# Attention scores and maxima as 128-row matmuls, the negated maximum as two of the rows

## The chip, the core and the metric

The kernel runs on one core of a Trainium2 chip as a single program. The metric is the device time of one execution in microseconds (us). Engines are named as the profile names them: PE is TensorE's matmuls and PEld its weight loads, DVE is VectorE, ACT is ScalarE, POOL is GpSimd, and SP is the engine whose queue issues nearly all DMAs.

## What is computed

A layer norm and an attention block with 16 heads of 16 dimensions over four sequences of 1024 tokens and 256 channels, then a ternary feed-forward, a memory layer that scans over the tokens, and the feed-forward again. The change touches only the softmax of the attention:

```python
qkv = (h @ w_qkv + b_qkv).reshape(B, T, 3, NUM_HEADS, HEAD_DIM)      # B 4, T 1024, 16 heads of 16
scores = jnp.einsum('bhqd,bhkd->bhqk', q, k) / np.sqrt(HEAD_DIM)
attn = jax.nn.softmax(scores, axis=-1)
out = jnp.einsum('bhqk,bhkd->bhqd', attn, v)
...
x = x + _L0_attn_a_ref(_layernorm(x, axis=-1), ...)
x = x + _L0_ffn_ref(_layernorm(x, axis=-1), L0_ffn_weight)
x = x + _L0_attn_b_ref(_layernorm(x, axis=-1), ...)
x = x + _L0_ffn_ref(_layernorm(x, axis=-1), L0_ffn_weight)
```

## The kernel before

**Numbers in two halves.** Queries and keys are kept as a rounded float32r part ("hi") and the rest ("lo"), written to DRAM (dq, dk) by `project`. A product of a query and a key is one float32r matmul with 64 rows: 16 dimensions times two parts of the query times two parts of the key. The 64 rows of one head stand in the slots by repeating the loads: `load_keys` writes each key row to two rows of a slot (`kslot`), `load_queries` does likewise for queries (`qslot`). Two heads (s = 0, 1) lie below each other in the 128 rows, and two such pairs (p = 0, 1) side by side, so that a slot holds four heads.

**Tiling.** A unit is one block of 256 queries (L34), one sequence b and two groups of four heads. A unit has two parts, one for each group; there are 32 units and 64 parts (L183 to L191). A part goes through the 1024 keys in eight steps kc of 128 keys. One such step is a call of `half` (L1219):

- `maxima` (L229) for a part that lies 12 steps ahead: two matmuls with queries as weights and 512 keys streaming, one for each half of the rows, into a tile of 1024 columns; then one VectorE reduction (L239) to the negated maximum over those keys. Eight such steps make a part's maxima.
- `scores` (L266): for the two pairs of heads, two matmuls each with 128 keys as weights and 256 queries streaming (L273), one for each half of the rows; then for each half a matmul of a matrix of ones with `mslot` (L278), which adds the negated maximum to the scores; then two exponentials on ScalarE (L281) into `pt`.
- `maxima_rows` (L241), once in eight steps: the eight negated maxima per query are split into two parts that sum to them, transposed, written to DRAM (d, four DMAs) and loaded into rows 0, 1 and 64, 65 of `mslot`, whose other rows are zero (two DMAs).

`weigh` (L285) then multiplies `pt` with the values: four float32 matmuls, each on 32 columns of the array; the machine runs a float32 matmul as two passes, so there are eight instructions. They accumulate over all steps of a unit in one PSUM bank (`av`), which VectorE copies out at the unit's end (L301), and `settle` divides by the softmax sums through DRAM.

**PSUM.** Of eight banks, four hold two maxima tiles, one `av`, and three rotate through all other work (`mps`, pool "m"): two for each step of scores before the change.

**What sets the order.** PE, DVE and ACT run in the order of the source text (`manual_schedule`, L975); SP and POOL are ordered by the framework. `part` (L1245) places the loads and calls `half` for each kc, then `beside(PACE)`, which issues pieces of the other work (projections of the next sequences, output projections, feed-forward, memory layer) up to an allowance counted in PE columns: 1200 per step, saved up to 1500, and at most 700 in one step once begun. After it come the value products: of this and earlier steps, if the other work was light (under 500 columns) or kc is odd.

```python
half(v, kc)
light = beside(PACE) < LIGHT
while late and (light or kc % 2):
    weigh_late()
late.append((v, kc))
```

**Slots and leads.** There are six key slots (three parts), four query slots and two for the maxima rows. In `part(v)`, keys are loaded at kc 1 and 5 (L1248, L1256), queries at kc 2 for part v + 3 (L1252), values at kc 2. A key slot serves both the maxima and, 12 steps later, the scores. `rest` (L1287) uses the slots as spare tiles when the attention has ended.

**The start.** `load_x`, constants, memsets of the slots that must hold zeros or ones (L1012 to L1016), then projection of the first sequence with loads in between (L1352 to L1359), then 12 steps of maxima alone.

Of the kernel before, what the change touches and what calls it, by code (L numbers as in the profile page):

```python
# [17 lines left out]
P = 128  # L18
# [3 lines left out]
SL = 32  # L22
# [15 lines left out]
def tile_hybrid(ctx: ExitStack, tc: tile.TileContext, x, ln_gamma, ln_beta, w_qkv, b_qkv, w_out, b_out,  # L38
# [22 lines left out]
    dq = [drk.tile([NG, 2, 2, HD, 2, S], F32, name=f"dq{b}") for b in range(B)]  # L61
    dk = [drk.tile([NG, 2, 2, 2, HD, S], F32, name=f"dk{b}") for b in range(B)]
# [114 lines left out]
    kslots = [slp.tile([P, 2, N5], F32R, tag=f"kslot{i}", name=f"kslot{i}") for i in range(6)]  # L177
    qslots = [slp.tile([P, 2, N5 // 2], F32R, tag=f"qslot{i}", name=f"qslot{i}") for i in range(4)]
    mslots = [slp.tile([P, N5], F32R, tag=f"mslot{i}", name=f"mslot{i}") for i in range(2)]
    ngs = [slp.tile([P, SL], F32, tag=f"ng{i}", name=f"ng{i}") for i in range(2)]  # L180
    ones = slp.tile([P, P], F32R, tag="ones", name="ones_r")
# [10 lines left out]
    W = N5 // 2  # L192
    vals, kS, qS = {}, {}, {}

    def load_keys(v, hf):

        if v >= len(parts) or (v, hf) in kS:
            return
        u, e = parts[v]
        k, b, gs = units[u]  # L200
        kt = kS[v, hf] = kslots[(2 * v + hf) % len(kslots)]
        src = dk[b][gs[e]].rearrange("p s h d n -> (s h d) p n")[:, :, hf * N5 : (hf + 1) * N5]
        to = kt.bitcast(F32).rearrange("(x r) p n -> x r p n", r=2)
        for r in range(2):
            nc.sync.dma_start(to[:, r], src)

    def load_queries(v):
# [7 lines left out]
        for s in range(2):  # L215
            src = dq[b][gs[e], :, s, :, :, t0 : t0 + W].rearrange("p d r n -> (d r) p n")
            for h in range(2):
                o = HR * s + SL * h
                nc.sync.dma_start(q.bitcast(F32)[o : o + SL], src)
# [9 lines left out]
    def maxima(v, n):  # L229

        hf, p, j = n // 4, n // 2 % 2, n % 2
        kt = kS[v, hf]
        if v not in nms:
            nms[v] = ngp.tile([P, 2, 2, 2, 2], F32, tag="nm", name=f"nm_{v}")
        ps = pools["x"].tile([P, 2, N5], F32, tag="x", name=f"mx_{v}_{n}")
        for s in range(2):
            r = slice(HR * s, HR * (s + 1))
            T.matmul(ps[:, s, :], lhsT=qS[v][r, p, j * P : (j + 1) * P], rhs=kt[r, p, :], start=True, stop=True)  # L238
        V.tensor_reduce(nms[v][:, hf, :, p, j], ps, AX.X, ALU.max, negate=True)  # L239

    def maxima_rows(v):  # L241
# [3 lines left out]
            out=nx, in0=nms[v][:, 0].rearrange("p s i j -> p (s i j)"),  # L245
# [728 lines left out]
    with ExitStack() as by_hand:  # L974
        by_hand.enter_context(tc.manual_schedule(engines=OWN))  # L975
        share(m=8)
        with ExitStack() as s1_:
# [35 lines left out]
            for t in mslots:  # L1013
                G.memset(t.bitcast(F32), 0.0)
# [426 lines left out]
```

## Time and profile before

| | us |
|---|---|
| median of 3 runs | 1516.4 (1515.99 to 1517.36) |
| the profiled execution | 1527.27 |
| its span, first to last instruction | 1525.5 |
| mean granted TensorE clock | 0.917 |

| stage of the profiled execution | us |
|---|---|
| before the first maxima | 0 to 52 |
| first score product to last | 72 to 1400 |
| the rest (end of the memory layer, outputs) | 1400 to 1525 |

A row of the page's costliest groups holds the line, the engine and operation, the tile written and those read, the shapes (`64*128` is rows times columns of the array in use), the count, the busy time of the group in us (overlaps counted once), the mean duration of one in ns, and the idle time of the engine just ahead of them with what ended it. A row of the timeline holds the start in us, the length of a run of equal instructions from first start to last end, engine, line, tiles, shape and count. Ends of matmuls are modelled, so that starts are what the intervals are read from. The granted clock (PEclk) is 1.00 or 0.50 at any moment.

The DMA engines moved 165.94 MB in 128657 packets and were busy 34.1% for the SP queue:

```profile
## 3 DMA queue, kind: packets, MB, share of 16 engines
q1 hardware_dynamic: 128252, 163.39, 34.1%
```

### The profile page before, as it was taken

The numbers are of one execution on the slowest core, as the hardware profiler recorded it, in microseconds if no ns is written. First come the engines' busy times: TensorE is split into PE (matmuls) and PEld (weight loads), VectorE is DVE, ScalarE is ACT, GpSimd is POOL, SyncE is SP. The second block draws the span as 40 slices with busy tenths as digits, with TensorE's granted clock in tenths as the row PEclk, the third lists the DMA queues.
The fourth block names the chain that finished last, engine by engine and source line by source line (L and its number), as shares of the span: only waits on it lengthen the run. The fifth ranks groups of instructions, "written<-read, shape, count | busy, mean of one in ns | idle before, by whom it ended". The sixth has DMA issues, their size and how long they took to land.

```text
span 1525.5 us, 27625 instructions
## 1 busy us (share of the span) xinstructions
PE 1333.4 (87%) x10496; PEld 790.4 (52%) x10496; DVE 1045.1 (69%) x1768; ACT 786.3 (52%) x1477; POOL 235.2 (15%) x434
## 2 busy tenths in 40 slices
PE   6469999999997897999988898999998888998786
PEld 3235455554554554655544554655545545654564
DVE  5656667587787657668778658678868568573564
ACT  2134536466666454566666454466654554565333
POOL 4331102000001103110002103110002113010233
PEclk9679999999999897999999898999998999999778
DMA  6536544544434222233443222334442222231001
GB/s 200 181 111 198 154 158 129 178 156 147 143 119 129 77 67 73 77 115 126 136 149 101 66 64 88 100 103 135 152 136 64 94 70 76 93 102 43 1 9 33
DMA packets 128657, 165.94 MB, mean 109 GB/s; under 512 B 33868, under 2 KB 76172, under 8 KB 128524
## 3 DMA queue, kind: packets, MB, share of 16 engines
q1 hardware_dynamic: 128252, 163.39, 34.1%
q8 instruction: 83, 1.36, 0.4%
q10 hardware_dynamic: 272, 0.79, 0.1%
q14 instruction: 50, 0.41, 0.1%
HBM read 123.24 MB, written 38.76 MB: 106 GB/s over the span
## 4 chain that ended last, share of the span: by engine, by line
PE 56%; DVE 22%; ACT 8%; DMA 6%; SPq 3%; issue 3%; POOL 2%; DVEq 0%; ACTq 0%; POOLq 0%
PE av L294 12%; PE mx L238 9%; DVE nm L239 8%; PE sc L273 6%; PE sc L278 6%; ACT pt L281 3%; PE cps L1139 2%; PE opf L874 2%; PE pf L390 2%; PE po L390 2%; DMA d<-nt 2%; PE gps L818 1%; PE vps L1162 1%; DMA dk<-lo 1%; PE qqps L540 1%
## 5 line engine op out<-in xcount | busy, mean ns | idle before, releaser
L281 ACT ACTIVATE pt<-sc 128x512 f32<-128x512 f32 x1024 | 555.7, 594 | 501.5 <-PE sc L278 500.0
L239 DVE TENSOR_REDUCE nm<-mx 128x2 f32<-128x1024 f32 x512 | 617.5, 1218 | 138.5 <-PE mx L238 131.6
L294 PE MATMUL av<-pt,v 128*32 128x256 f32 x4096 | 333.9, 413 | 30.3 <-DVE a L301 30.2
L238 PE MATMUL mx<-kslot,qslot 64*128 64x512 f32 x1024 | 275.1, 520 | 26.4 <-DVE lo L1144 15.3
L273 PE MATMUL sc<-qslot,kslot 64*128 64x256 f32 x2048 | 237.1, 295 | 27.6 <-DVE kqm L634 14.8
L273 PEld LDWEIGHTS sc<-qslot,kslot 64*128 64x128 f32 x2048 | 220.7, 196 | 59.1 <-ACT pt L281 19.2
L278 PE MATMUL sc<-mslot,ones_r 64*128 64x512 f32 x1024 | 226.2, 412 | 15.5 <-DMA mslot<-d 15.3
L238 PEld LDWEIGHTS mx<-kslot,qslot 64*128 64x128 f32 x1024 | 102.8, 191 | 249.8 <-issue 129.9
L294 PEld LDWEIGHTS av<-pt,v 128*32 128x32 f32 x4096 | 91.2, 112 | 169.5 <-issue 114.0
L278 PEld LDWEIGHTS sc<-mslot,ones_r 64*128 64x128 f32 x1024 | 113.7, 196 | 18.5 <-DMA mslot<-d 9.9
L72 POOL TENSOR_TENSOR rso_hn<-rsi_hn,nhalf 128x2 f32<-128x2 f32 (+1 forms) x17 | 11.9, 699 | 332.0 <-DVE rsi_hn L71 332.0
L1139 PE MATMUL cps<-hT,wg 128*128 128x512 f32 x128 | 62.6, 629 | 0.1
L1144 DVE SCALAR_TENSOR_TENSOR lo<-cps,bqk,hi 128x512 fp32r<-128x512 f32 x32 | 23.9, 751 | 54.8 <-ACT hi L1143 44.4
L1143 ACT ACTIVATE hi<-cps,bqk 128x512 fp32r<-128x512 f32 x32 | 22.0, 688 | 51.8 <-PE cps L1139 26.1
L1139 PEld LDWEIGHTS cps<-hT,wg 128*128 128x128 f32 x128 | 23.9, 199 | 28.5 <-issue 25.7
L874 PE MATMUL opf<-ffn,ohT 128*128 128x256 f32 x128 | 33.2, 404 | 5.1 <-ACT ohT L869 5.1
L72 POOL TENSOR_TENSOR rso_hd<-rsi_hd,nhalf 128x2 f32<-128x2 f32 (+1 forms) x17 | 11.9, 700 | 158.8 <-DVE rsi_hd L71 146.7
L1180 POOL TENSOR_SCALAR X<-X,rr_a 128x256 f32<-128x256 f32 x32 | 18.6, 591 | 111.7 <-DVE h L1121 111.7
L557 DVE SCALAR_TENSOR_TENSOR vk<-rvk,cw_vk,vk 128x512 f32<-128x512 f32 x21 | 15.8, 752 | 28.5 <-ACT vk L555 28.0
L390 PE MATMUL po<-wo,aT 128*128 128x256 f32 x128 | 35.2, 419 | 0.0
L818 PE MATMUL gps<-gwT,hid 128*128 128x256 f32 x128 | 33.7, 408 | 0.5 <-ACT pt L281 0.5
L301 DVE COPY a<-av 128x512 f32<-128x512 f32 x32 | 21.8, 683 | 16.7 <-PE av L294 16.6
(358 smaller groups left out, 1583.6 us busy)
## 6 DMA issues: line engine op xcount, KB each, us to landing
kslot<-dk SPq DMA_DIRECT2D x256, 256.0 KB
v<-dv SPq DMA_DIRECT2D x32, 604.0 KB
qslot<-dq SPq DMA_DIRECT2D x256, 64.0 KB
da<-a SPq DMA_DIRECT2D x31, 256.0 KB
dv<-vtile SPq DMA_DIRECT2D x8, 604.0 KB
X<-in_L_attn_a_x_dram SPq DMA_DIRECT2D x8, 512.0 KB
dq<-hi SPq DMA_DIRECT2D x16, 256.0 KB
dq<-lo SPq DMA_DIRECT2D x16, 256.0 KB
```

The source lines that it names most:

```text
L72: G.tensor_tensor(out=r[:, :n], in0=t[:, :n], in1=nhalf[:, :n], op=ALU.pow)
L238: T.matmul(ps[:, s, :], lhsT=qS[v][r, p, j * P : (j + 1) * P], rhs=kt[r, p, :], start=True, stop=True)
L239: V.tensor_reduce(nms[v][:, hf, :, p, j], ps, AX.X, ALU.max, negate=True)
L273: T.matmul(ps[s][:, p * W : (p + 1) * W], lhsT=kt[r, p, o : o + P], rhs=qS[v][r, p, :], start=p == 0, stop=False, skip_group_check=True,)
L278: T.matmul(ps[s], lhsT=ones[r, :], rhs=mslots[v % 2][r, :], start=False, stop=True, skip_group_check=True)
L281: A.activation(pt[:, s, :], ps[s], AF.Exp, scale=1.0 / HD**0.5)
L294: T.matmul(avs[u][SL * i : SL * (i + 1), e * W : (e + 1) * W], lhsT=vt[:, kc, o : o + SL], rhs=pt[:, i % 2, i // 2 * W : (i // 2 + 1) * W] ...
L390: T.matmul(ps[:, e, :], lhsT=srcT[:, cc, e, :], rhs=w[:, cc, :], start=cc == 0, stop=cc == 1)
L818: T.matmul(ps[:, e, :], lhsT=hidT[:, cc, p.start + e, :], rhs=gwT[:, cc, :], start=cc == 0, stop=cc == 1)
L874: T.matmul(pf[:, e, :], lhsT=hT[:, cc, e, :], rhs=ffn[:, cc, :], start=cc == 0, stop=cc == 1)
L1139: T.matmul(ps, lhsT=wg[:, cc, n * P : (n + 1) * P], rhs=hT[:, cc, o], start=cc == 0, stop=cc == 1)
L1144: V.scalar_tensor_tensor(out=low, in0=ps, scalar=bqk[:, n : n + 1], in1=high.bitcast(F32), op0=ALU.add, op1=ALU.subtract,)
```

## The change

Line numbers ahead are those of the kernel before. Each head now has the array's 128 rows for itself: 64 rows of products as before, two rows (64 and 65) in which the query slot holds the two parts of the negated maximum and the key slot for scores holds ones, and 62 rows of zeros. So one matmul gives a score with its maximum taken off, and the separate product with the matrix of ones (L278) is gone. For maxima the key slot must hold zeros in rows 64 and 65, so keys are loaded twice, into `mslots` (two heads, 512 keys) for maxima and `sslots` (four heads, 256 keys) for scores, three slots of each, each load issued as two DMAs two pieces ahead of its use, inside `maxima` and `scores`. Query slots hold four heads side by side; there are three, loaded for part v + 2 at kc 0. DRAM layouts of dq and dk follow. `maxima_rows` writes its rows into the query slot with one load.

The order in a step changes: `scores` stand ahead of `maxima`; a step's scores go bank by bank, two products and an exponential each. Value products are issued at odd kc, and at kc 0 of a unit's first part, for all steps that are left. `PACE` is 600, `LIGHT` is gone. At the start nine slots are cleared and three pairs of rows set to one.

```diff
-    dq = [drk.tile([NG, 2, 2, HD, 2, S], F32, name=f"dq{b}") for b in range(B)]
-    dk = [drk.tile([NG, 2, 2, 2, HD, S], F32, name=f"dk{b}") for b in range(B)]
+    dq = [drk.tile([NG, 4, HD, 2, S], F32, name=f"dq{b}") for b in range(B)]
+    dk = [drk.tile([NG, 4, 2, HD, S], F32, name=f"dk{b}") for b in range(B)]
...
-    kslots = [slp.tile([P, 2, N5], F32R, tag=f"kslot{i}", name=f"kslot{i}") for i in range(6)]
-    qslots = [slp.tile([P, 2, N5 // 2], F32R, tag=f"qslot{i}", name=f"qslot{i}") for i in range(4)]
-    mslots = [slp.tile([P, N5], F32R, tag=f"mslot{i}", name=f"mslot{i}") for i in range(2)]
+    W = N5 // 2
+    qslots = [slp.tile([P, 4, W], F32R, tag=f"qslot{i}", name=f"qslot{i}") for i in range(3)]
+    sslots = [slp.tile([P, 4, W], F32R, tag=f"sslot{i}", name=f"sslot{i}") for i in range(3)]
+    mslots = [slp.tile([P, 2, N5], F32R, tag=f"mslot{i}", name=f"mslot{i}") for i in range(3)]
...
-    ones = slp.tile([P, P], F32R, tag="ones", name="ones_r")
...
+    def keys_into(t, of):
+
+        to = t.bitcast(F32)[:HR].rearrange("(x r) i n -> x r i n", r=2)
+        for r in range(2):
+            nc.sync.dma_start(to[:, r], of.rearrange("i h d n -> (h d) i n"))
+
+    def load_scored(x):
+
+        v, c = x // 4, x % 4
...
+        scored[x] = sslots[x % len(sslots)]
+        keys_into(scored[x], dk[b][gs[e], :, :, :, c * W : (c + 1) * W])
+
+    def load_maxed(y):
+
+        v, hf, p = y // 4, y // 2 % 2, y % 2
...
+        maxed[y] = mslots[y % len(mslots)]
+        keys_into(maxed[y], dk[b][gs[e], 2 * p : 2 * p + 2, :, :, hf * N5 : (hf + 1) * N5])
...
-        for s in range(2):
-            src = dq[b][gs[e], :, s, :, :, t0 : t0 + W].rearrange("p d r n -> (d r) p n")
-            for h in range(2):
-                o = HR * s + SL * h
-                nc.sync.dma_start(q.bitcast(F32)[o : o + SL], src)
+        src = dq[b][gs[e], :, :, :, t0 : t0 + W].rearrange("i d r n -> (d r) i n")
+        for h in range(2):
+            nc.sync.dma_start(q.bitcast(F32)[SL * h : SL * (h + 1)], src)
...
         hf, p, j = n // 4, n // 2 % 2, n % 2
-        kt = kS[v, hf]
+        if j == 0:
+            load_maxed(4 * v + n // 2 + 2)
+        kt = maxed[4 * v + n // 2]
...
         for s in range(2):
-            r = slice(HR * s, HR * (s + 1))
-            T.matmul(ps[:, s, :], lhsT=qS[v][r, p, j * P : (j + 1) * P], rhs=kt[r, p, :], start=True, stop=True)
+            T.matmul(
+                ps[:, s, :], lhsT=qS[v][:, 2 * p + s, j * P : (j + 1) * P], rhs=kt[:, s, :], start=True, stop=True
+            )
...
-        for s in range(2):
-            nc.sync.dma_start(
-                mslots[v % 2].bitcast(F32)[HR * s : HR * s + 2, :], d[:, s].rearrange("h x q -> h (x q)")
-            )
+        nc.sync.dma_start(
+            qS[v].bitcast(F32)[HR : HR + 2].rearrange("h i n -> h (i n)"), d.rearrange("h x q -> h (x q)")
+        )
...
-        kt, o = kS[v, kc // 4], kc % 4 * P
-        ps = [mps([P, N5], f"sc_{v}_{kc}_{s}") for s in range(2)]
-        rows = [slice(HR * s, HR * (s + 1)) for s in range(2)]
-        for p in range(2):
-            for s, r in enumerate(rows):
+        if kc % 2 == 0:
+            load_scored(4 * v + kc // 2 + 2)
+        kt, o = scored[4 * v + kc // 2], kc % 2 * P
+        pt = pts[v, kc] = ptp.tile([P, 2, N5], F32, tag="pt", name=f"pt_{v}_{kc}")
+        for x in range(2):
+            ps = mps([P, N5], f"sc_{v}_{kc}_{x}")
+            for y in range(2):
                 T.matmul(
-                    ps[s][:, p * W : (p + 1) * W], lhsT=kt[r, p, o : o + P], rhs=qS[v][r, p, :],
-                    start=p == 0, stop=False, skip_group_check=True,
+                    ps[:, y * W : (y + 1) * W], lhsT=kt[:, 2 * x + y, o : o + P], rhs=qS[v][:, 2 * x + y, :],
+                    start=True, stop=True,
                 )
-        for s, r in enumerate(rows):
-            T.matmul(ps[s], lhsT=ones[r, :], rhs=mslots[v % 2][r, :], start=False, stop=True, skip_group_check=True)
-        pt = pts[v, kc] = ptp.tile([P, 2, N5], F32, tag="pt", name=f"pt_{v}_{kc}")
-        for s in range(2):
-            A.activation(pt[:, s, :], ps[s], AF.Exp, scale=1.0 / HD**0.5)
+            A.activation(pt[:, x, :], ps, AF.Exp, scale=1.0 / HD**0.5)
...
-            G.memset(ones.bitcast(F32), 1.0)
-            for t in mslots:
+            for t in (*qslots, *mslots, *sslots):
                 G.memset(t.bitcast(F32), 0.0)
+            for t in sslots:
+                G.memset(t.bitcast(F32)[HR : HR + 2], 1.0)
...
-            LIGHT, PACE = 500, 1200
+            PACE = 600
...
                 pend = None
+                if v is not None:
+                    scores(v, kc)
                 if todo:
...
-                if v is not None:
-                    scores(v, kc)
...
-                    if kc == 1:
-                        load_keys(v + 2, 1)
-                    if kc == 2:
-                        if v + 3 < 2 * n0:
-                            through("before", lambda key: key <= units[(v + 3) // 2][1])
-                        load_queries(v + 3)
-                        if v % 2 == 0 and v // 2 + 1 < U:
-                            load_values(v // 2 + 1)
-                    if kc == 5:
-                        load_keys(v + 3, 0)
+                    if kc == 0:
+                        b = units[min(v // 2 + 1, U - 1)][1]
+                        if v + 2 < 2 * n0 and b:
+                            through("before", lambda key: key <= b)
+                        load_queries(v + 2)
+                    if kc == 4 and v % 2 == 0 and v // 2 + 1 < U:
+                        load_values(v // 2 + 1)
                     half(v, kc)
-                    light = beside(PACE) < LIGHT
-                    while late and (light or kc % 2):
-                        weigh_late()
+                    beside(PACE)
+                    if kc % 2 or v % 2 == 0 and kc == 0:
+                        while late:
+                            weigh_late()
                     late.append((v, kc))
...
-                for v in (2 * u, 2 * u + 1):
-                    load_queries(v)
-                    for hf in range(2):
-                        if v < 3:
-                            load_keys(v, hf)
+                if u == 0:
+                    for v in range(2):
+                        load_queries(v)
+                    for y in range(3):
+                        load_maxed(y)
+                    for x in range(3):
+                        load_scored(x)
```

## The prediction

> **What bounds the kernel now.** I read the page's head first, then its costliest groups, then one stretch of TensorE in order of time, then busy times by stretch, and last the SP queue.
>
> ```profile
> span 1525.5 us, 27625 instructions
> PE 1333.4 (87%) x10496; PEld 790.4 (52%) x10496; DVE 1045.1 (69%) x1768; ACT 786.3 (52%) x1477; POOL 235.2 (15%) x434
> ...
> L239 DVE TENSOR_REDUCE nm<-mx 128x2 f32<-128x1024 f32 x512 | 617.5, 1218 | 138.5 <-PE mx L238 131.6
> L294 PE MATMUL av<-pt,v 128*32 128x256 f32 x4096 | 333.9, 413 | 30.3 <-DVE a L301 30.2
> L238 PE MATMUL mx<-kslot,qslot 64*128 64x512 f32 x1024 | 275.1, 520 | 26.4 <-DVE lo L1144 15.3
> L273 PE MATMUL sc<-qslot,kslot 64*128 64x256 f32 x2048 | 237.1, 295 | 27.6 <-DVE kqm L634 14.8
> ...
> L278 PE MATMUL sc<-mslot,ones_r 64*128 64x512 f32 x1024 | 226.2, 412 | 15.5 <-DMA mslot<-d 15.3
> ```
>
> TensorE is busy 87% of the span and hardly waits for data: the idle times ahead of its four big groups add up to 100 us. All four belong to one step, which I call a half: 512 halves, each with one maxima pair (L238), four score products (L273), two products that add the negated maximum (L278) and eight value products (L294). One half in order of time (start, duration, line, count):
>
> ```profile
> 700.89 0.50 PE L238 MATMUL mx<-kslot,qslot 64*128 64x512 f32 x2
> 701.22 0.41 PE L273 MATMUL sc<-qslot,kslot 64*128 64x256 f32 x4
> 701.46 0.40 PE L278 MATMUL sc<-mslot,ones_r 64*128 64x512 f32 x2
> 701.79 0.64 PE L294 MATMUL av<-pt,v 128*32 128x256 f32 x8
> 702.36 0.50 PE L238 MATMUL mx<-kslot,qslot 64*128 64x512 f32 x2
> ```
>
> The starts tell what each group costs: 0.33 + 0.24 + 0.33 + 0.57 = 1.47 us. Four score products of 256 columns in 0.24 us are two pairs at 0.12 each, so the two 64-row tiles run at the same time. A 512-column pair should then take 0.22; the two that stand next to a change of tile shape (L238 behind `128*32`, L278 ahead of it) take 0.33, that is 0.11 more. Busy times of whole stretches (length; PE, PEld, DVE, ACT, POOL busy; granted clock, DMA share, GB/s):
>
> ```profile
> 736.50:748.60 12.10, 12.10 (x132) 6.66 (x131) 10.98 (x14) 8.69 (x17) 0.00 (x0) 1.00 0.59 193
> 597.00:614.00 17.00, 15.60 (x89) 10.52 (x91) 12.16 (x26) 5.98 (x12) 3.88 (x8) 0.50 0.14 43
> 100.00:1400.00 1300.00, 1190.08 (x9900) 694.67 (x9899) 925.26 (x1482) 731.04 (x1372) 163.81 (x288) 0.94 0.36 112
> ```
>
> The first is one part (8 halves) with hardly any other work beside it: PE full, VectorE at 91%, the DMA engines at 59%. I counted 22 of the 64 parts shorter than 16.2 us like it; the others carry projections and memory work, and PE is the bound there too.
>
> **The change, part by part.** *Streaming.* The 64-row pairs become single 128-row matmuls, one after another, and the L278 pair goes. Removed per half: 0.23 (L238, without the 0.11 for its change of shape) + 0.24 (L273) + 0.22 (L278) = 0.69 us. Added: four products of 256 columns and two of 512, in the same type. No 128-row matmul of this type is in the trace. From below, a pair's time for a single one: 4 x 0.12 + 2 x 0.22 = 0.90 us. From above, the float32 passes that do fill the array:
>
> ```profile
> 299.74 3.62 PE L1162 MATMUL vps<-wg,hT 128*128 128x256 f32 x16
> 114.56 9.99 PE L1139 MATMUL cps<-hT,wg 128*128 128x512 f32 x22
> ```
>
> Less the last one's own duration (0.38 and 0.59), these come every 0.216 us (256 columns) and 0.45 us (512), so a half would need 4 x 0.216 + 2 x 0.45 = 1.76 us. I take the lower one: the type sets the rate, since a float32 pass on `64*128` (L833, 256 columns) also starts every 0.215 us. 0.90 - 0.69 = 0.21 us a half, times 512: **+107 us**; bounds +84 (0.107 and 0.213 per product, half the float32 pass) and +548.
>
> The Trainium skill speaks against this part: "TensorE: Matmul & The Clock Gate", Part 3 (row/col tiling), states that a weight load overlaps a running matmul only where the row groups differ, and in a full array they never do. The two rows above disagree: twice the columns cost twice the time (0.45 against 0.216), so no constant weight load is in them. By the rule, with a load of 0.107 us (an estimate from that page's columns / 1.2 GHz), six loads in 512 halves would add 329 us more; the trace decides.
>
> *Changes of tile shape.* Scores and maxima now have the shape of most projections (`128*128`), and value products are issued for two halves together. In the two listed orders of instructions the shape changes 1141 times before and 715 times after, between the first maxima and the last value product. Entering `128*32` costs 0.11 + 0.02 (its first pass takes 0.24 instead of 0.22); leaving it 0.09 of drain + 0.11 of exposed weight load, 0.20; the other kinds about 0.20. Before: 429 x 0.13 + 712 x 0.20 = 198 us. After: 287 x 0.13 + 428 x 0.20 = 123 us. **-75 us**; bounds -55 and -89 (all 426 at 0.13, or at 0.21).
>
> *Negated maxima as rows of the query slot.* The chain nx, transpose, d (4 DMAs), one load instead of two (0.25 us less) stays. The rows are now needed by a half's first product and no more by L278, 0.57 us later, and the last reduction starts 0.45 us later since maxima stand behind scores. PE waited for these rows 16 times, 25.2 us in all. **+5 us** (16 times 0.3); bounds 0 and +40 (0.6 in every part). What waits behind it on PE is the rest of the half, and VectorE's reductions.
>
> *Keys loaded twice, in small pieces.* Issue times on SP (min/median/max in ns):
>
> ```profile
> L205 SPq DMA_DIRECT2D kslot<-dk x256: 580/610/1651, 35.3 to 1355.8; - x128
> L219 SPq DMA_DIRECT2D qslot<-dq x256: 303/427/1441, 32.1 to 1340.1; - x128
> ```
>
> Per part, 4 x 0.61 + 4 x 0.43 + 2 x 0.25 = 4.7 us go and 16 key loads, 2 query loads and 1 row load come: 18 x 0.52 + 0.25 = 9.6 us (0.52 is midway between the two medians: rows are strided as for kslot, but half as many), 5.7 to 11.2 at 0.30 and 0.61 each. In the 12.1 us part SP was issuing for 7.5 us by the trace; it will be at 12.4 (8.5 to 14.0). The bytes of keys per part go from 1 to 2 MB, +87 GB/s there: 193 to 280, so the DMA share goes from 0.59 to about 0.86. And a load is issued only 4 halves (5.9 us) ahead of its use, in a slot that the piece just finished had; before, 7 for keys. Behind a late key load wait, on SP, the d and query-row loads, and on PE everything. Elsewhere a part lasts 20 to 30 us and covers this. **+8 us** (0.36 in each of 22 parts); bounds 0 and +55 (2.5 in each).
>
> *At the start* POOL clears nine slots of 1024 columns and three pairs of rows: from the 128x512 rows (0.49 each) 8.8 + 2.9 us instead of 1.2, where it idled 9.29 us before L1097 (the first statistics). **+1 us**; bounds 0 and +3.
>
> *Cover and pace.* ACT's two exponentials and VectorE's reduction per half are unchanged: 1.08 and 1.22 us, still below 1.49. Other work beside a half is halved in pace (600 for 1200 columns) but all of it is still issued before the end: the PE columns after the last value product are the same (37402 and 37403). Spread thinner, it may spare waits for the copy L301 (30.2 us) or cause some in the projections, which now run in larger bursts. **0**; bounds -30 and +15.
>
> Sum: 107 - 75 + 5 + 8 + 1 = **+46 us** at rounded prices. The profiled execution took 1527.3 us, 1.8 around its span, so it would take 1573; it stands 10.9 above the median of the runs, 1516.4. The forecast for the median is 1516.4 + 46 = **1562 us**.
>
> **The rivals.** *A, faster: the clock.* Between 100 and 1400 us the granted clock is 0.94, so some 12% of 1300 us ran at half speed, costing up to 78 us. The stretch from 597 shows how: PE had idled, then worked 17 us at 0.50, while a full part has 1.00. Fewer shape changes, thinner other work and more streaming could keep it up. It decides from 0.98 on: at that, 0.04 x 1300 = 52 us come back, and 1562 - 52 = 1510; at 0.99, 1497. Against it: those stretches come from waits for VectorE's chain in the memory work, which stays. The same page of the skill, Part 1, states that the clock is halved after an idle window of about 3.4 us; if no stall of that kind went, nothing would come back.
>
> *B, slower by more: SP and the DMA engines become the bound of the short parts.* At the upper price +55 instead of +8: 1609. For it: 62% of SP's time and 59% of the DMA engines are used there already. Against it: 42 parts have time to spare.
>
> *C: the 128-row product of this type streams at the float32 pass's rate.* +548 in place of +107: about 2000. Against it, the pairs' 0.12.
>
> *D: shape changes cost more than priced*, at -89, and streaming the least, +84: 1516.4 - 5 + 14 = 1525.
>
> **How the numbers follow.** The forecast, 1540 to 1590: 0.48. D, 1519 to 1540: 0.12. B: 0.14. C: 0.02. A: 0.19. That leaves 0.05 within 0.2% (3 us), which is about what a measurement of this kernel can tell from no change. Faster 0.19, same 0.05, slower 0.76. The range leaves out C, the best of A and the worst of B: 1505 to 1610.
>
> **What would show it.** Right: score products of 256 columns start every 0.11 to 0.12 us, maxima every 0.22; a lone half at about 1.49 us against 1.47, and halves with projections shorter than before; SP busy nine tenths or more in short parts; waits of PE for the DMAs of the key slots, few and short. Wrong: products at 0.22 (C); weight loads standing between matmuls; a mean clock of 0.98 or more between 100 and 1400 us (A); PE waiting over 1 us for key slots in most short parts (B); or the shape change being dearer than 0.2 us.

## The result, and the profile after

The changed kernel takes 1657.2 us (median of 4 runs, 1654.4 to 1671.4) against 1516.2 for the kernel before: a ratio of 1.0947, 95% interval 1.0894 to 1.1001. The forecast was 1562 us, slower: the direction was right, but the forecast loss of 46 us is a third of the measured 141, and the time lies outside the range.

The profiled execution has a span of 1669.6 us. The head of its page and its costliest groups of PE and DVE:

```profile
span 1669.6 us, 26853 instructions
PE 1403.6 (84%) x9472; PEld 917.4 (55%) x9472; DVE 1046.0 (63%) x1768; ACT 779.0 (47%) x1477; POOL 248.6 (15%) x443
...
L254 DVE TENSOR_REDUCE nm<-mx 128x2 f32<-128x1024 f32 x512 | 617.6, 1218 | 317.4 <-PE mx L251 316.3
L289 PE MATMUL sc<-qslot,sslot 128*128 128x256 f32 x2048 | 407.8, 320 | 76.5 <-DMA sslot<-dk 49.0
L251 PE MATMUL mx<-mslot,qslot 128*128 128x512 f32 x1024 | 347.5, 423 | 68.6 <-DMA mslot<-dk 39.9
L306 PE MATMUL av<-pt,v 128*32 128x256 f32 x4096 | 296.8, 404 | 11.1 <-DVE a L313 11.1
```

The two key slots now head the waits of the groups that had hardly any. Two halves in order of time, the value products of two halves first:

```profile
808.00 1.07 PE L306 MATMUL av<-pt,v 128*32 128x256 f32 x16
809.00 0.74 PE L289 MATMUL sc<-qslot,sslot 128*128 128x256 f32 x4
809.57 0.63 PE L251 MATMUL mx<-mslot,qslot 128*128 128x512 f32 x2
810.04 0.71 PE L289 MATMUL sc<-qslot,sslot 128*128 128x256 f32 x4
810.59 0.62 PE L251 MATMUL mx<-mslot,qslot 128*128 128x512 f32 x2
```

Here nothing waits. From one group of 16 value products to the next such a pair of halves takes 3.16 us at the median (51 pairs at full clock), 1.58 a half against 1.47 before. Over 512 halves that would be some 55 us, so the matmuls alone are not the loss. The longest PE waits that name a DMA, in us, times and the longest one:

```profile
PE sc L289 <- DMA sslot<-dk: 49.0, 27, 4.0
PE mx L251 <- DMA mslot<-dk: 39.9, 43, 3.1
PE vkps L552 <- DMA hid<-dh: 35.3, 3, 11.9
```

The issues on SP, and the queue's share of the 16 DMA engines (34.1% before):

```profile
L199 SPq DMA_DIRECT2D mslot<-dk x512: 571/598/2948, 38.3 to 1512.1; - x171
L199 SPq DMA_DIRECT2D sslot<-dk x512: 571/602/1762, 42.3 to 1533.0; - x171
```

```profile
q1 hardware_dynamic: 203772, 230.54, 49.2%
```

All but 5 us of the loss lie between the first score product and the last: 71.8 to 1399.6 before, 76.9 to 1543.9 after; what follows takes 125.9 and 125.7 us. I cut this loop into its 64 parts at every 32nd score product, and the sums below, worked out from the records of single profiled executions, serve all that follows. "First" are parts 0 to 10, with the projections; "light" the other 20 that lasted under 16.2 us before; "mid" 12 up to 22 us; "heavy" 18 longer ones, and 20, 36, 52 the three in which a block of the memory layer begins. Idle is time without a matmul; "half speed" is length times (1 - granted clock), part by part. (A stall can count in both.)

| loop, us | all | first | light | mid | heavy | 20, 36, 52 | PE idle | half speed |
|---|---|---|---|---|---|---|---|---|
| before | 1328 | 258 | 285 | 231 | 487 | 68 | 127 | 89 |
| after | 1467 | 288 | 386 | 239 | 435 | 120 | 196 | 104 |
| e1, no reloads | 1289 | 246 | 326 | 222 | 418 | 78 | 81 | 31 |
| e5, before, no reloads | 1314 | 253 | 285 | 229 | 478 | 68 | 123 | 79 |
| e7, before, new pace | 1342 | 260 | 325 | 223 | 418 | 117 | 165 | 73 |
| e8, before, extra loads | 1448 | 268 | 324 | 288 | 501 | 67 | 216 | 136 |
| e17, before, allowance 600 | 1310 | 256 | 299 | 238 | 448 | 69 | 112 | 87 |
| e10, e1 with the old order | 1322 | 248 | 307 | 218 | 485 | 64 | 85 | 30 |
| e18, e1, value products spread | 1322 | 253 | 326 | 222 | 453 | 68 | 78 | 45 |

After against before: light parts +102, the three parts +52, the first 11 +30, heavy parts -53.

### The profile page after: what moved, and what is told of

Read it like the earlier page. It is cut to its first block, busy times and chain, and to the rows that moved or that the text cites. A ratio compares the mean times of both kernels' runs of the same rounds, so it can differ in the third digit from the quotient of the medians.

```text
span 1669.6 us, 26853 instructions
## 1 busy us (share of the span) xinstructions
PE 1403.6 (84%) x9472; PEld 917.4 (55%) x9472; DVE 1046.0 (63%) x1768; ACT 779.0 (47%) x1477; POOL 248.6 (15%) x443
## 4 chain that ended last, share of the span: by engine, by line
PE 54%; DMA 15%; DVE 13%; SPq 6%; ACT 5%; POOL 4%; issue 3%; DVEq 0%; ACTq 0%; POOLq 0%
PE sc L289 12%; PE mx L251 10%; PE av L306 9%; DMA mslot<-dk 6%; DVE nm L254 5%; SPq L199 4%; DMA sslot<-dk 3%; PE pf L402 2%; PE cps L1152 2%; PE vps L1175 2%; PE opf L886 2%; DMA da<-a 2%; PE gps L830 1%; PE po L402 1%; ACT pt L293 1%
## 5 line engine op out<-in xcount | busy, mean ns | idle before, releaser
L289 PE MATMUL sc<-qslot,sslot 128*128 128x256 f32 x2048 | 407.8, 320 | 76.5 <-DMA sslot<-dk 49.0
L289 PEld LDWEIGHTS sc<-qslot,sslot 128*128 128x128 f32 x2048 | 307.9, 198 | 244.3 <-issue 147.9
L251 PE MATMUL mx<-mslot,qslot 128*128 128x512 f32 x1024 | 347.5, 423 | 68.6 <-DMA mslot<-dk 39.9
L306 PE MATMUL av<-pt,v 128*32 128x256 f32 x4096 | 296.8, 404 | 11.1 <-DVE a L313 11.1
L251 PEld LDWEIGHTS mx<-mslot,qslot 128*128 128x128 f32 x1024 | 167.0, 200 | 84.9 <-issue 41.4
L72 POOL TENSOR_TENSOR rso_hn<-rsi_hn,nhalf 128x2 f32<-128x2 f32 (+1 forms) x17 | 14.6, 860 | 386.6 <-DVE rsi_hn L71 386.6
L552 PE MATMUL vkps<-hid,wvk 128*128 128x512 f32 x32 | 21.9, 823 | 35.3 <-DMA hid<-dh 35.3
L72 POOL TENSOR_TENSOR rso_hd<-rsi_hd,nhalf 128x2 f32<-128x2 f32 (+1 forms) x17 | 11.9, 702 | 223.7 <-DVE rsi_hd L71 210.7
L1175 PE MATMUL vps<-wg,hT 128*128 128x256 f32 x128 | 34.3, 423 | 8.4 <-DVE lo L1157 8.4
L402 PE MATMUL pf<-ffn,hnT 128*128 128x256 f32 x124 | 39.7, 477 | 0.5 <-ACT hnT L395 0.5
L1175 PEld LDWEIGHTS vps<-wg,hT 128*128 128x128 f32 x128 | 27.0, 214 | 16.1 <-DVE lo L1157 10.8
L402 PEld LDWEIGHTS pf<-ffn,hnT 128*128 128x128 f32 x124 | 30.1, 246 | 8.3 <-ACT pt L293 1.3
```

The costliest lines, as they stand in the source:

```text
L72: G.tensor_tensor(out=r[:, :n], in0=t[:, :n], in1=nhalf[:, :n], op=ALU.pow)
L251: T.matmul(ps[:, s, :], lhsT=qS[v][:, 2 * p + s, j * P : (j + 1) * P], rhs=kt[:, s, :], start=True, stop=True)
L289: T.matmul(ps[:, y * W : (y + 1) * W], lhsT=kt[:, 2 * x + y, o : o + P], rhs=qS[v][:, 2 * x + y, :], start=True, stop=True,)
L306: T.matmul(avs[u][SL * i : SL * (i + 1), e * W : (e + 1) * W], lhsT=vt[:, kc, o : o + SL], rhs=pt[:, i // 2, i % 2 * W : (i % 2 + 1) * W], ...
L402: T.matmul(ps[:, e, :], lhsT=srcT[:, cc, e, :], rhs=w[:, cc, :], start=cc == 0, stop=cc == 1)
L1175: T.matmul(ps[:, e, :], lhsT=hT[:, cc, o : o + P], rhs=wg[:, cc, 2 * C :], start=cc == 0, stop=cc == 1,)
```

## The experiments

Times are medians, followed by the ratio and its 95% interval. Ratios are to the kernel before in the same session, so compare ratios; 0.01 is 15 us.

**How much the key loads cost (e1, e2, e3, on the changed kernel).** e1 loads the slots for the first three pieces alone and leaves the later loads of keys out; e2 loads half of the columns with as many DMAs; e3 issues only the first of each two DMAs, and so leaves out the products with the queries' lower parts.

```diff
 # e1, for sslots; mslots likewise with y
+        if x < 3:
+            keys_into(scored[x], dk[b][gs[e], :, :, :, c * W : (c + 1) * W])
 # e2
+            n = of.shape[-1] // 2
+            nc.sync.dma_start(to[:, r, :, :n], of[:, :, :, :n].rearrange("i h d n -> (h d) i n"))
 # e3
-        for r in range(2):
+        for r in range(1):
```

> The changed kernel (1657 us) with only the first three pieces of each kind of key slot loaded; all later pieces reuse what lies there, so scores and maxima are of the wrong keys (the work on every engine but the DMAs is the same). Theory 'late keys': what is left of the change is TensorE's own part, +107 streaming and -75 shape changes and small terms, so 1530 to 1570. Rival 'TensorE and pacing': the loss is in streaming, shape changes and the new order of the other work, and 1620 or more stays.

> The changed kernel with the same number of key loads, each moving only the first half of its columns (half the bytes; the other half of a slot keeps zeros or old values, so scores and maxima are wrong there). If the DMA engines' bandwidth makes keys late: 1580 to 1610. If SP's issue time or the short lead does: 1630 to 1657, nearly no change.

> The changed kernel with one of the two DMAs of each key load left out (odd rows of the key slots stay zero, so the products are wrong): half the bytes, as in the run before, and half of SP's key issues, 8 fewer per part. If SP's issue time is the limit: 1550 to 1590, well below the run with half the bytes. If bytes are: the same as that run within 10 us.

e1: 1490.1 us, 0.9775 (0.9728 to 0.9821). e2: 1590.2, 1.0434 (1.0374 to 1.0494). e3: 1543.4, 1.0123 (1.0075 to 1.0170). e1 is below both forecasts, e2 in the band of bandwidth, e3 below the band of issue time. From 1.0947, half the bytes give back 0.051, half the issues another 0.031, the rest of the loads 0.035: 0.117 or 178 us in all. Both cost, bytes and the number of DMAs. e3 moves the bytes of e2 with half the key issues, but also in 147 thousand packets instead of 204 thousand; which of the two saves the 0.031 is not separated. With the later loads left out the changed kernel beats the one before.

Light part 32 shows how. Windows of the whole loop and of that part (busy times of PE, PEld, DVE, ACT, POOL; granted clock, DMA share, GB/s), first of the changed kernel:

```profile
100.00:1400.00 1300.00, 1119.25 (x7825) 721.78 (x7825) 830.08 (x1314) 636.86 (x1198) 143.26 (x249) 0.93 0.53 148
825.90:845.80 19.90, 15.98 (x113) 9.53 (x113) 10.71 (x13) 8.58 (x16) 0.00 (x0) 0.83 0.64 172
```

and of e1:

```profile
100.00:1400.00 1300.00, 1208.40 (x8853) 793.76 (x8851) 929.89 (x1500) 720.74 (x1372) 175.54 (x303) 0.97 0.21 63
719.30:733.60 14.30, 13.08 (x117) 8.22 (x113) 11.17 (x14) 8.37 (x16) 0.00 (x0) 1.00 0.34 103
```

The part takes 19.9 us instead of 14.3, with the DMA engines at 64% on average; in stretches of 2 us they go from 0.13 to 1.00. The SP queue of the changed kernel in it, in order of time:

```profile
834.35 1.09 SPq L331 DMA_DIRECT2D aT<-da  x2
835.54 1.26 SPq L199 DMA_DIRECT2D mslot<-dk  x2
837.24 1.71 SPq L271 DMA_DIRECT2D d<-nt  x4
838.99 0.42 SPq L237 DMA_DIRECT2D v<-dv  x1
840.48 0.23 SPq L274 DMA_DIRECT2D qslot<-d  x1
840.76 1.24 SPq L199 DMA_DIRECT2D sslot<-dk  x2
```

and PE:

```profile
841.34 1.07 PE L306 MATMUL av<-pt,v 128*32 128x256 f32 x16
845.77 0.36 PE L289 MATMUL sc<-qslot,sslot 128*128 128x256 f32 x1 [3.36 <-DMA sslot<-dk]
```

The load for the next part's keys, the third of this part, stands in SP's order behind all of these. From 834.4 to 840.8 SP mostly issues; some 1.5 us are gaps, in which it waits for VectorE's work on d and for d's own landing. The load is issued at 840.8, PE needs it at 842.4 and starts at 845.8. Of its lead of four halves 1.6 us are left, and with the engines at 0.85, 0.76 and 0.58 in the three stretches of 2 us from 840 on it takes 5 us to land.

**Was the load on the queue enough by itself? (e5, e8, e9, on the kernel before.)** e5 leaves out the loads of keys from part 3 on. e8 adds eight 128 KB copies of keys to each part from part 3 on, DRAM to DRAM, that nobody reads, and keeps the long leads; e9 cuts these to 8 columns.

```diff
 # e5
+        if v < 3:
+            for r in range(2):
+                nc.sync.dma_start(to[:, r], src)
 # e8; e9 with hf * N5 : hf * N5 + 8, and :8 on the left
+        for c in range(4 if v > 2 else 0):
+            of = dk[b][gs[e], c // 2].rearrange("s h d n -> (h d) s n")[:, :, hf * N5 : (hf + 1) * N5]
+            nc.sync.dma_start(extra[(8 * v + 4 * hf + c) % 16].rearrange("(x r) s n -> x r s n", r=2)[:, c % 2], of)
```

> The kernel before with keys loaded for the first three parts only (later parts reuse the slots, so scores are of the wrong keys). It is the like-for-like partner of the changed kernel without reloads (1490 us, its own before 1525). If keys were never late in the kernel before: 0.99 to 1.00 of before, and TensorE's part of the change is then a gain of 1 to 2%. If the reloads cost the kernel before as well: 0.97 to 0.98, and TensorE's part is about nothing, as near to the forecast +33 us as it gets.

> The kernel before with eight more DMAs of 128 KB per part (keys copied from DRAM to a scratch tensor in DRAM that nobody reads), so 12 key DMAs and 2 MB per part where it had 4 and 1 MB; leads unchanged at 7 halves. If the load on SP and on the DMA engines makes keys late by itself: 1.03 or more. If only the short lead of the changed kernel does: 1.00 to 1.01.

> The kernel before with eight more DMAs per part, on the same queue and of the same rows as e8's, but of 8 columns instead of 512: 488 DMAs of 2 KB that nobody reads. e8, with 128 KB each, took 1646.6 us (+8.4%). Theory 'bytes' (the waiting loads stand behind bulk data on the DMA engines): the time is that of the kernel before, 1515 to 1530 us. Theory 'issue' (SP's queue is the bound, some 0.55 us for each DMA whatever its size, 4.4 us in a part): most of e8's loss stays, 1600 us or more. In between, the share (time - 1520) / 126 is what issuing costs by itself.

e5: 1518.6, 0.9993 (0.9966 to 1.0020): keys were never late before. e8: 1646.6, 1.0836 (1.0773 to 1.0899). e9: 1554.9, 1.0225 (1.0181 to 1.0268), between the theories: issuing, with small packets in the place of large ones, is 0.27 of e8's loss, the bytes the rest. A small DMA occupies SP as long as a large one; in e8

```profile
L209 SPq DMA_DIRECT2D extra<-dk x488: 534/596/2442, 82.1 to 1484.7; - x163
```

and in e9

```profile
L209 SPq DMA_DIRECT2D extra<-dk x488: 528/595/1680, 82.4 to 1269.8; - x163
```

No key was late in e8. What waited longer were loads with no lead at all, the rows of the maxima and hid. Before and in e8:

```profile
PE sc L278 <- DMA mslot<-d: 15.3, 6, 7.7
PE vkps L540 <- DMA hid<-dh: 9.3, 3, 3.4
```

```profile
PE sc L282 <- DMA mslot<-d: 68.6, 21, 7.7
PE vkps L544 <- DMA hid<-dh: 42.1, 6, 11.7
```

**Order and pace alone (e6, e7, on the kernel before).** e7 takes the new allowance and the value products at odd steps; e6 puts scores ahead of maxima as well.

```diff
-            LIGHT, PACE = 500, 1200
+            PACE = 600
...
-                    light = beside(PACE) < LIGHT
-                    while late and (light or kc % 2):
-                        weigh_late()
+                    beside(PACE)
+                    if kc % 2 or v % 2 == 0 and kc == 0:
+                        while late:
+                            weigh_late()
```

> The kernel before (64-row pairs, one load of keys, ones product) with the changed kernel's order alone: scores ahead of maxima, allowance 600, value products at odd kc. If the changed kernel's gain on TensorE comes from its order and batching: 0.97 to 0.99 of before. If it comes from the 128-row shape that spares shape changes with the projections: 0.995 to 1.02.

> As the run before, but with maxima ahead of scores as in the kernel before: only the allowance of 600 and the value products at odd kc. If the order of scores and maxima matters: over 0.5% from that run. If only pace and batching do: the same within 0.5%.

e6: 1563.8, 1.0306 (1.0253 to 1.0359). e7: 1541.3, 1.0167 (1.0106 to 1.0228). e6 is slower than both of its forecasts, and the order of scores and maxima does matter, 0.014 between the two. On 64 rows the new order and pace are a loss; but the table shows that they move time: from before to e7 the heavy parts get 70 us shorter, the light parts 41 longer and the three parts 49 longer.

**Another queue, fewer DMAs (e4, e11, e12, on the changed kernel).** e4 issues the loads for maxima from POOL's queue; e11 stores each key row twice in DRAM, so that one DMA of 64 rows fills a piece (the projections write 32 DMAs more); e12 does both.

```diff
 # e4 and e12, in load_maxed
-        keys_into(maxed[y], ...)
+        keys_into(maxed[y], ..., G)
 # e11
-        for r in range(2):
-            nc.sync.dma_start(to[:, r], of.rearrange("i h d n -> (h d) i n"))
+        by.dma_start(t.bitcast(F32)[:HR], of.rearrange("i h d r n -> (h d r) i n"))
```

> The changed kernel with the key loads for maxima issued from POOL instead of SP; bytes, pieces and leads unchanged. If SP's queue (issue time and what blocks in it) is the limit: 1570 to 1610. If bytes or the lead of four halves are: 1645 to 1665. If POOL's own queue blocks the loads or its issue is dearer: slower than 1665.

> The changed kernel with keys stored in DRAM with each row twice, so that a piece is loaded by one DMA of 64 rows instead of two of 32: the same bytes into the slots, the same lead, 8 instead of 16 key DMAs in a part (and 32 writes more in the projections). From half the bytes alone to half the bytes with half the DMAs (e2 to e3) the time fell by 47 us. Theory 'issue counts beside bytes': 1595 to 1625 us instead of 1657. Theory 'bytes alone': 1645 us or more. If the issue of a DMA of 64 rows takes twice that of one of 32 (1.1 instead of 0.57 us), nothing is gained by either theory, and the row of SP's issues shows it.

> e11 with the loads for the maxima issued by POOL instead of SP (this change alone took 29 us off the changed kernel, e4). If queueing on SP is still a bound after e11: 15 to 30 us below e11. If e11 has freed SP already: within 8 us of e11. With all bytes still moved, no theory has it below the kernel before (1516 us) unless bytes cost nothing.

e4: 1628.2, 1.0663 (1.0608 to 1.0717), 43 us less than the changed kernel by the ratios, between the theories. e11: 1646.5, 1.0845 (1.0790 to 1.0900): 0.010 less, at the edge of the band of bytes alone, although a DMA of 64 rows took SP no longer (0.58 us) and issues had counted in e3 and e9. Its packets were slower: those of 2 KB took 161 ns at the median, against 84 in the changed kernel, which can hide what the issues saved. e12: 1640.6, 1.0799 (1.0767 to 1.0832). That is 7 us from e11 by the ratios, as forecast if e11 had freed SP already. In e12 no wait for hid is left and those for the key slots are 13.8 us (89 in the changed kernel), but the rows of the maxima are the new wait:

```profile
PE sc L287 <- DMA qslot<-d: 91.8, 25, 8.2
```

So with all bytes moved the wait changes its name and stays. A freer SP doesn't help the light parts either: SP issues for 10.7 us of one in e4 and 10.2 in e11 against 15.5 in the changed kernel (means of parts 11 to 50), and the 20 light parts still take 378 and 371 us against 386.

**The three long parts (e13 on the changed kernel, e14 on e7).** In part 20 of the changed kernel the last write of dh is issued at 541.4 us. SP after it, with 14 DMAs ahead of the load of hid:

```profile
541.36 1.21 SPq L426 DMA_DIRECT2D dh<-hdT  x2
542.67 1.03 SPq L231 DMA_DIRECT2D qslot<-dq  x2
543.75 1.27 SPq L199 DMA_DIRECT2D sslot<-dk  x2
545.12 1.22 SPq L199 DMA_DIRECT2D mslot<-dk  x2
546.44 0.53 SPq L327 DMA_DIRECT2D da<-a  x1
547.07 1.23 SPq L199 DMA_DIRECT2D sslot<-dk  x2
549.33 0.56 SPq L329 DMA_DIRECT2D dn<-da  x1
549.93 1.10 SPq L331 DMA_DIRECT2D aT<-da  x2
551.13 1.26 SPq L199 DMA_DIRECT2D mslot<-dk  x2
552.43 0.58 SPq L525 DMA_DIRECT2D hid<-dh  x1
```

PE stands at the first product that needs hid from 545.8 to 557.4. Windows of the stall, of what follows and of what comes then:

```profile
545.80:557.40 11.60, 0.01 (x1) 0.04 (x1) 1.56 (x2) 0.45 (x1) 0.00 (x0) 0.68 0.66 216
557.40:565.00 7.60, 6.70 (x34) 3.56 (x35) 2.63 (x4) 3.65 (x7) 0.19 (x1) 0.81 0.36 125
565.00:572.00 7.00, 7.00 (x43) 3.97 (x41) 6.26 (x11) 4.39 (x8) 0.81 (x2) 1.00 0.18 53
```

A stall is paid twice: 11.6 us idle, then 2 x 0.19 x 7.6 = 2.9 us at half speed, which cost 1.4 more. The edit of both runs:

```diff
-        nc.sync.dma_start(t, dh[c])
+        G.dma_start(t, dh[c])
```

> The changed kernel with the load of hid (6 DMAs in the attention loop) issued by POOL's queue instead of SP's. Theory 'place in SP's queue': SP issues 15 other DMAs between the last write of dh and this load (541.4 to 552.4 us in part 20), so three stalls of some 12 us shrink to 3 or 4 each: 25 to 35 us less than the changed kernel, 1620 to 1635 us, and parts 20, 36 and 52 last 26 to 30 us instead of 40. Theory 'bytes': the load, issued early, lands late all the same, and the time stays within 8 us of 1657.

> The kernel before with the new pace (e7: allowance of 600, value products at odd steps; 1541 us) and the load of hid from POOL's queue. In e7 the parts 20, 36 and 52 together last 117 us against 68 before, and TensorE waits 30.9 us there for hid<-dh, while all other parts together are 35 us shorter than before. Theory 'place in SP's queue': 1500 to 1515 us, as fast as the kernel before or up to 1% faster. Theory 'bytes': 1535 us or more.

e13: 1632.5, 1.0775 (1.0725 to 1.0825), 26 us less than the changed kernel by the ratios, as forecast; but the waits for hid fall only from 35.3 to 14.6 us, and the three parts to 32 to 35 each, not to 26 to 30. e14: 1518.6, 0.9996 (0.9975 to 1.0017), 26 us less than e7; waits for hid 30.9 to 7.3 us. The place in the queue is the larger part of these stalls, the landing the rest. e14 misses its band by 4 us; the next runs show why.

**Which half of the pace (e15, e16, e17, on the kernel before).** e17 has only the allowance of 600; e15 that and hid on POOL's queue; e16 only the latter.

```diff
-            LIGHT, PACE = 500, 1200
+            LIGHT, PACE = 500, 600
```

> The kernel before with the allowance of 600 columns alone, value products as before, and the load of hid from POOL's queue. If the allowance brings the shorter heavy parts (418 us in e7 against 487 before, for 18 parts), heavy parts stay at 415 to 435 us here, and the time is within 1% of e14 (more changes of tile shape, 1129 against 874, cost 255 x 0.13 to 0.2 us or 33 to 51 us of TensorE time, of which the parts bound by other engines hide some: up to 30 us slower than e14). If the gathered value products bring them, heavy parts are at 470 us or more.

> The kernel before with the load of hid from POOL's queue and nothing else. TensorE waited 9.3 us for hid<-dh in the kernel before, in all. If e15's 18 us come from this load: 1500 us. If they come from the allowance: 1510 to 1520 us.

> The kernel before with the allowance of 600 columns alone, the load of hid on SP's queue. If e15's 18 us come from the allowance and POOL's queue only spares the new stalls in parts 20, 36 and 52: between 1501 and 1535 us, with these three parts at 80 us or more together (69 in e15, 117 in e7). If the stalls of e7 came from the gathered value products and not from the allowance: the three parts stay at 70 us and the time at 1500 us.

e15: 1500.5, 0.9894 (0.9856 to 0.9933). e16: 1520.8, 1.0000 (0.9972 to 1.0028). e17: 1501.5, 0.9869 (0.9825 to 0.9914): one number, 1200 to 600, makes a kernel that beats both, about 20 us below the one before, and the other queue for hid adds nothing that shows. In e17 the three parts stay at 69 us, so the stalls of e7 came with the gathered value products. These cost the 64-row kernel 18 us (e14 against e15). PE's wait for ScalarE's exponentials says where, in e15 and then in e14:

```profile
PE sc L273 <- ACT pt L281: 8.8, 6, 2.3
```

```profile
PE sc L273 <- ACT pt L281: 43.8, 101, 1.4
```

PE stands ahead of scores until ScalarE has freed a bank. That the two banks of a step, both held until the L278 products are done, make this, is argued and not tried.

**TensorE's part on 128 rows (e10, e18, both e1 with an edit).** They leave out the later loads of keys as e1 does. e10 has the whole order of the kernel before; e18 only its rule for the value products, with the allowance of 600 and scores first.

> e1 (the changed kernel with key slots loaded for the first three pieces alone; 1490 us, granted clock 0.953) with the order of the kernel before: maxima ahead of scores, an allowance of 1200 columns, value products of a step at once where the other work was light. It leaves out the later loads of keys. Theory 'order' (the 33 us that TensorE's part gained against the kernel before without reloads, 1518.6 us, come from the order and the pace): 1515 to 1530 us. Theory 'shape' (they come from 128-row products without the separate product for the maximum): 1475 to 1495 us, and no more than 1% from e1, since the same order cost the kernel before 1.7 to 3.1% the other way.

> e1 (changed kernel, key slots loaded for the first three pieces alone, so it leaves out the later loads of keys; 0.9775 of the kernel before) with the value products issued as in the kernel before, at once where the other work was light; allowance 600 and scores ahead of maxima stay. The tile shape changes 974 times instead of 715. By the prediction's price (259 x 0.13 to 0.2 us) it takes 34 to 52 us more than e1: 1.000 to 1.012 of the kernel before. If gathering costs as much as it saves, as on 64 rows (e14 against e15, 18 us more): 0.965 to 0.98.

e10: 1525.0, 1.0033 (1.0016 to 1.0050). e18: 1520.9, 1.0017 (0.9991 to 1.0043). e1 stands at 0.9775, so on 128 rows gathering saves 0.024 or 37 us for 259 changes of tile shape, 0.14 us each, as e18's expectation had it. At full clock two lone halves take 3.41 us in e18 and a gathered pair 3.15 in e1, 0.13 a change; over the loop 14 of the 33 us between the two rows of the table are half speed. On 64 rows gathering costs time, and there PE waits for the exponentials; here that wait is 14.1 us in e18 and 13.0 in e1.

## Why the prediction was wrong

**Streaming, +107: right.** Products of 256 columns start every 0.117 us and those of 512 every 0.234. From the first maxima product to the value products takes 1.13 us in e10 and 0.90 in e5, some 0.225 a half or 115 us. (4 x 0.12 + 2 x 0.22 is 0.92 and not 0.90, so the prediction's own prices give +118.) Rival C is out. So is, for these products, the rule of the Trainium skill that was weighed, "TensorE: Matmul & The Clock Gate", Part 3 (a weight load overlaps only where the row groups differ): the weight loads of these full-array products take 0.19 us by the records, and the products still follow each other in 0.117.

**Changes of tile shape, -75: the price held at its low end, the term was a little large.** 426 x 0.13 to 0.14 is 55 to 60. A half takes 1.58 and not 1.49: its products need 4 x 0.117 + 2 x 0.234 = 0.94 where the sum has 0.90, and in the scores that stand behind maxima one of the four starts 0.08 late, with its weight load. By the loop's table (all less idle less half speed) PE's work grew by 55 us from before to after, 65 from e5 to e1, where the two terms gave 32.

**Cover and pace, 0 (-30 to +15), and rival A: each half right.** Without late loads the idle time falls from 123 to 81 us and the half-speed loss from 79 to 31 (e5 to e1), 90 us. PE's stops of over 1.5 us between 100 and 1360 us fall from 24 to 8. Windows of e5, e10 and e1:

```profile
100.00:1360.00 1260.00, 1154.37 (x9668) 677.68 (x9664) 912.71 (x1465) 710.93 (x1336) 164.29 (x281) 0.95 0.21 64
100.00:1360.00 1260.00, 1176.22 (x8464) 778.58 (x8460) 903.96 (x1434) 698.58 (x1307) 168.38 (x282) 0.98 0.21 64
100.00:1360.00 1260.00, 1180.12 (x8725) 776.05 (x8724) 917.24 (x1468) 707.20 (x1347) 170.92 (x290) 0.98 0.21 64
```

The clock and the cover do not come from the pace: e10, with the order and pace of the kernel before, already has the 0.98, 85 us of idle time and 30 at half speed. They came with the rest of the change, the 128-row products and what goes with them. A lone half lasts 1.70 us there against 1.47, beside the same work of VectorE and ScalarE; that this covers their waits is argued and not tried. By itself it only pays for the streaming (e10 1.0033, e5 0.9993). The new order and pace then take 33 us off, 30 of them PE's own work (e10 to e1), and without the gathering nearly nothing of that is left (e18). So TensorE's part of the change was a gain of 0.022 or 33 us, where the prediction's sum without the loads was +38: the sign was wrong. Rival A had the mechanism and its clock, 0.98; in the changed kernel, with the late loads, the clock is 0.93.

**Keys loaded twice, +8 (0 to +55): the step that failed.** It cost 178 us (after against e1), 3 times the upper bound and 22 times the value. Three sentences of it fell. "0.36 in each of 22 parts" and the bound of 2.5 counted SP's busy time against the part's length, as if the queue were a pipe that is late only when it is full. That time was put too low, 12.4 us (8.5 to 14.0) where SP issued for 15.1 in part 32, for which it was worked out; a key load holds SP for 0.60 us and not 0.52. But SP was not full (busy 0.68 to 0.84 of the light parts up to part 50), nor were the DMA engines on average (0.64 in part 32), and with a third of SP's issuing gone the light parts stay as long (e4, e11): a load is late by what waits ahead of it in SP's order and by the bytes ahead of it on the engines. "Elsewhere a part lasts 20 to 30 us and covers this" was wrong for the same reason: of the 178 us, the loop's table puts 60 in the light parts, 42 in the first 11 (PE waits 23 us for key slots there, and 8.4 against 1.3 for projections that stand behind the writes of dq and dk), 41 in parts 20, 36 and 52, and the rest in the others. And "Behind a late key load wait, on SP, the d and query-row loads" named one of the two victims, hid not, and gave no price: e8, in which keys have their long lead, loses 0.084 with 90 us more idle time, 53 of it for d's rows and 33 for hid. So the short lead wasn't needed for a loss of this size, though in the changed kernel 89 us of the waits are for keys; a longer lead there was not tried. Rival B named SP and the DMA engines, and its +55 for the short parts is near the 60 that the light parts lost, though neither was full there; "42 parts have time to spare", which spoke against it, left out the other 118. As each late load stops PE, it also takes the clock: of the 178 us, e1 and after differ by 115 in idle time and 73 at half speed, with some of it in both.

The same page of the skill, Part 1, states that the clock is halved after an idle window of about 3.4 us. Part 20 agrees: at 0.68 over 11.6 us it ran at half speed for the last 7.4 (2 x 0.32 x 11.6), so from 4.2 us after the stop. Most drops of the clock had no such stop ahead of them. Between 100 and 1400 us it fell 30 times in the changed kernel, 27 of them with no stop of PE of 3.3 us or more in the 8 us ahead, by the records. In the kernel before it fell 27 times, and the longest such stop was 3.0 us. So the prediction's "if no stall of that kind went, nothing would come back" fell too: in e1 the clock came back as the shorter stops went.

**Negated maxima, +5, and POOL's memsets, +1: small.** PE waits 3.7 us for the query rows in the changed kernel and 23.3 in e1, against 15.3 for their likes before (the prediction's 25.2 adds 9.9 of PEld's own waits). The first score product is 5.1 us later, 76.9 against 71.8, above the bound of 3; how much of it is POOL's is not shown.

Open: what makes PE wait for the exponentials when value products are gathered on 64 rows and not on 128; how much of the cost of many small DMAs is SP's issuing and how much their packets; and how much of the gain would stay if keys were loaded once on 128 rows with right values, since the slots for 12 steps of them don't fit beside the rest and this wasn't tried.

## What to carry over

Price added DMAs not by the queue's busy share but by the loads with no lead that share the queue: list every small load that PE waits for within a few us of its issue (a round trip through DRAM, a tile just written), and what will stand ahead of it. Ask of every part of a mixed change what it does alone: here a setting that went along with the change, an allowance halved, beats both kernels by itself. A stall of TensorE costs more than its length, since the clock falls behind it, and it falls behind short stops too.

## What the runs showed of the hardware

- A DMA of the same rows holds SP's queue for 0.595 us whether it moves 2 KB or 128 KB (e9, e8), and one of 64 adjacent rows no longer (0.58) than one of 32 rows two apart (0.60).
- With the DMA engines busy 0.50 of the time between 100 and 1400 us in e8, 0.53 in the changed kernel and 0.63 in e12, TensorE still waited up to 7.7 us (e8) and 8.2 us (e12) for the rows of the maxima, and 11.9 us for hid (the changed kernel).
- Storing key rows twice and loading 64 adjacent rows by one DMA (e11) took the packets of 2 KB from 84 to 161 ns at the median.
- 488 DMAs of 2 KB cost 34 us (e9), 488 of 128 KB cost 127 us (e8), though neither had a reader.
- The granted clock was halved 27 times between 100 and 1400 us of the kernel before, with no stop of TensorE over 3.0 us in the 8 us ahead of any of them.
